# Rows by token from the first experts on: expert results combined and normed by token, residuals of feed-forward blocks added by the vector engine, the last attention by token

## The chip, the cores and the metric

The kernel runs on one core of one Trainium2 chip. The metric is device time in microseconds (us), as the median of several executions. TensorE (PE) multiplies matrices, VectorE (DVE), ScalarE (ACT) and GpSimd (POOL) work on tiles, and SyncE (SP) issues most DMAs. An indirect DMA (a gather or scatter of rows by index) is issued by POOL.

## The reference, cut to what matters

Eight sequences of 256 tokens with 128 channels (2048 tokens) go through eight sublayers; each is followed by an addition of its input and a layer norm.

```python
x = _layernorm(x + rglru(x)); x = _layernorm(x + local_attention(x)); x = _layernorm(x + mamba(x))
x = _layernorm(x + _L1_ffn_ref(x, ...))     # 32 experts, one per token
x = _layernorm(x + _L2_attn_ref(x, ...))    # chunked attention, below
x = _layernorm(x + _L2_ffn_ref(x, ...))     # 8 routed experts, two per token, and a shared one
x = _layernorm(x + _L3_attn_ref(x, ...))    # causal attention with 16 heads of four types
x = _layernorm(x + _L3_ffn_ref(x, ...))     # x @ w_eff.T + bias, w_eff ternary

def _L1_ffn_ref(x, ...):
    ...
    out_tok = jnp.where(accepted[:, None], out_tok * gate[:, None], 0.0)
    return (xt + out_tok).reshape(B, S, H)

def _L2_attn_ref(x, ...):
    # _layernorm here has a scale g and a bias b per channel
    def _mha(x, wqs, wks, wvs, pw, pb, g, b):
        ...
        return _layernorm(out @ pw + pb + x, g, b)
    def _ffn(x, w1, b1, w2, b2, g, b):
        h = jax.nn.relu(x @ w1 + b1)
        return _layernorm(h @ w2 + b2 + x, g, b)
    # la: heads within chunks of 32 tokens; sa: the same across chunks
    x = _mha(x, la...); x = _ffn(x, lf...); x = regroup(x)
    x = _mha(x, sa...); x = _ffn(x, pf...); return regroup_back(x)

def _L2_ffn_ref(x, ...):
    ...
    routed = jnp.zeros_like(xf).at[dispatch.reshape(-1)].add(contrib.reshape(-1, h))
    shared = jax.nn.silu(x @ sg) * (x @ su) @ sd
    return shared + SCALE * routed.reshape(b, s, h)
```

Since the first experts' sublayer returns x + g·out and is added to x again, the norm there is of 2x + g·out.

## The kernel before, in words

A tensor lies in SBUF either by channel (128 partitions are the channels, tokens run along the row) or by token (128 partitions are tokens, `z[128, 2, 128]` for one sequence). Matmuls contract over partitions, so they want their input by channel. A norm over channels is a norm along the row when a tensor lies by token; when it lies by channel the mean needs a matmul.

- `layernorm_steps` (L426 to L456) norms a tensor by channel. Its short form makes the centred tensor by one matmul with `centre` (tile ln), ACT squares it, a second matmul with `mean` gives the variance in the same tile, ACT forms exp(-0.5·ln(var + eps)) (ln_rs, two instructions of 256 columns) and DVE multiplies. Its form in steps has ln_mean (PE), ln_xc (DVE, L446), ln_sq (ACT, L448), ln_var (PE), ln_rs (ACT, L453 and L454) and the product (DVE, L456), with a `yield` between groups.
- `normed` (from L1240) norms by token: per 128 tokens DVE's bn_stats (L1246) and bn_aggr (L1247), then two ACT instructions of two columns (rs, L1249 and L1250), then DVE subtracts and multiplies (z, L1253). `by_channel` (L1256) transposes z back on PE (tile zt, L1259).
- `chunked` (L1348) works on the eight sequences one by one: attention la, feed-forward lf, attention sa, feed-forward pf. `on_pe` (L277) interleaves three sequences at a time: each is a generator that yields (its PE cost, the time until its next PE work can start), and the generator whose due time comes first issues next. So the order of each engine's queue is settled when the program is built.
- In `chunked`, `gather` fetches the first experts' results by token (got; three sequences ahead, issued by POOL at L1122). `combined` multiplies them by the gate (DVE, L1384), transposes them (PE, back, L1385), adds twice the layer's input by channel (DVE, xc, L1390) and norms by channel.
- `ffn` (from L1325) puts bias and residual into the output bank by PE: `add_bias` is a bf16 matmul of three bias rows against ones (out<-bias_rows), and `x` times the identity (out<-ident) adds the residual. `mha` adds its bias in the same way.
- `moe2` runs the shared expert in four parts of 512 tokens: `shared(0)` first, then the eight routed experts, then parts 1 to 3. For each of eight slices of the hidden width pg and pu are made, ACT and DVE form sh, and `acc` (by channel, 128x512) accumulates. `results(b)` takes two gathered rows per token, weights and sums them on DVE (L1551, L1553), transposes them (L1554), adds the shared part (L1556) and norms by channel to x_moe, the last attention's input. 32 gathers are issued after the experts.
- `typed` is the last attention and the ternary linear layer. A list of units (48 for the 8 sequences) gives PE's order by hand; between units up to three side steps are taken from a queue of generators: `results` of a later sequence, its projections (`typed_before`), and `after(b, o)` of a finished one: wo (L394 through `mm`), residual (L1734), norm in steps, lin, bias and residual (L1740), norm in steps, store. One PSUM bank (tag M) serves the side steps.

All matmuls made through `mm` have the line L394 in the profile. The first layers (rglru, local attention, mamba, up to about 917 us) and the first experts themselves are not touched, but for a smaller load of bias rows.

Of the kernel before, what the change touches and what calls it, by code (L numbers as in the profile page):

```python
# [21 lines left out]
P = 128  # L22
# [132 lines left out]
def _layout(d):  # L155
# [81 lines left out]
    rows = np.zeros((96, 4, P), f)  # L237
    rows[::32] = np.stack([d["L2_attn_" + n] for n in ("la_pb", "lf_b2", "sa_pb", "pf_b2")])
    out["b2"] = rows.reshape(96, 4 * P)
# [57 lines left out]
class _Kernel:  # L297
# [128 lines left out]
    def layernorm_steps(self, pool, src, dst, eps=EPS, tag="ln", steps=False):  # L426
# [29 lines left out]
        nc.vector.tensor_mul(dst, xc, rs)  # L456

# [491 lines left out]
    def route1(self, t0, t1, pools, small):  # L949
# [65 lines left out]
        nc.vector.tensor_scalar(pos, pos, float(CAP), None, ALU.is_le)  # L1015
# [104 lines left out]
    def gather(self, pool, buf, get, t, tag, bufs=None):  # L1120
        r = pool.tile([P, P], F32, tag=tag, name="got", **({"bufs": bufs} if bufs else {}))
        self.nc.gpsimd.indirect_dma_start(  # L1122
            out=r,
            out_offset=None,
            in_=buf,
            in_offset=bass.IndirectOffsetOnAxis(ap=get[:, t : t + 1], axis=0),
        )
        return r
# [9 lines left out]
    def moe1(self):  # L1138
        nc, tc = self.nc, self.tc
        E, CAP = 32, 80  # L1140
        with (
# [3 lines left out]
            full = one.tile([96, 4 * P], F32, name="bias_full")  # L1145
# [77 lines left out]
    def bias_rows(self, pool, full):  # L1223

        nc = self.nc
        self.bias = self.fc.tile([96, 4, P], BF, name="bias_rows")
        flat = self.bias.rearrange("p i d -> p (i d)")
        part = pool.tile([96, 4 * P], BF, name="bias_part")
# [96 lines left out]
    def ffn(self, x, w, name, bias, work, small):  # L1325
# [12 lines left out]
        self.add_bias(out, bias)  # L1338
        for t in range(2):
            ts = slice(t * P, (t + 1) * P)  # L1340
            for c in range(4):
                self.mm(out[:, t, :], h[:, c, ts], w2[:, c, :], False, False)
            self.mm(out[:, t, :], x[:, ts], self.ident, False, t == 1)
        z = self.normed(out[:, 0:2, :], work, small, "z")
# [3 lines left out]
    def chunked(self):  # L1348
# [7 lines left out]
        with (  # L1356
# [15 lines left out]
            def results(b):  # L1372
                got.extend(self.gather(work, self.ybuf1, self.get1, 2 * b + j, "got", 6) for j in range(2))
# [3 lines left out]

            def combined(b):

                ps = self.psum("B", "back")  # L1380
                for j in range(2):
                    t = 2 * b + j
                    r = got[t]
                    nc.vector.tensor_scalar(r, r, self.gate1[:, t : t + 1], None, ALU.mult)  # L1384
                    nc.tensor.transpose(ps[:, j * P : (j + 1) * P], r, self.ident)  # L1385
                if b + 3 < B:
                    assert len(got) == 2 * b + 6
                    results(b + 3)
                s = work.tile([P, S], F32, tag="xc", name="xc", bufs=1)
                self.combined = nc.vector.scalar_tensor_tensor(s, self.x[:, bass.ts(b, S)], 2.0, ps[:, 0:S], ALU.mult, ALU.add)  # L1390
                yield 0.3, 1.0
                x = work.tile([P, S], F32, tag="xb", name="x_moe1", bufs=5)
                self.layernorm(work, s, x)
                yield 0.9, 2.5
# [4 lines left out]
            def one_sequence(b):  # L1399
# [9 lines left out]
                x1 = affine(z, "la", "x1")  # L1409
                yield 0.3, 0.6  # L1410
                z = yield from self.ffn(x1, w[:, 0, :], "lf", 1, work, small)
                x2 = affine(z, "lf", "x2", there)
                yield 0.3, 0.6
                z = yield from self.mha(x2, self.fws[1], self.m("blk8"), 2, work, small, pools)
                x3 = affine(z, "sa", "x1")
# [3 lines left out]
                z = yield from self.ffn(x3, w[:, 1, :], "pf", 3, work, small)  # L1419
# [15 lines left out]
                self.logits(b, y, self.w1[:, 866:874], self.lg2[:, 2 * b : 2 * b + 2, :])  # L1435
                assert self.routed == b
# [9 lines left out]
            self.routed = 0  # L1446
            on_pe([one_sequence(b) for b in range(B)], 3, [self.typed_weights(prep)])
# [22 lines left out]
    def moe2(self):  # L1470
# [9 lines left out]
        with (  # L1480
# [5 lines left out]
            def shared(i):  # L1486
                cs = bass.ts(i, 512)
                acc = self.psum("S", "acc")
                for c in range(8):
# [4 lines left out]
                    i = nc.scalar.activation(h, pg, AF.Silu)  # L1494
                    if self.norm:

                        self.issue_after([i], self.norm)
                        self.norm = None
                    self.silu = i
# [317 lines left out]
```

## Time and profile before

| | us |
|---|---|
| median of 3 runs | 1902.89 (1902.8 to 1905.53) |
| the profiled execution's own time | 1898.62 |
| its span | 1896.8 |
| PE busy, granted clock | 1585.0 (84%), 0.91 |
| DVE, ACT, POOL busy | 1093.2, 1020.7, 560.4 |
| chunked attention | about 950 to 1437 |
| second experts | 1437 to 1625 |
| last attention and linear layer | 1625 to 1897 |

A row of a group names line, engine, operation, output<-input, shape and count, then the busy time in us, the mean duration of one in ns, the idle time of the engine just before these instructions, and what ended it. PEld is the load of a stationary operand. A row of a window names its bounds, its length, each engine's busy time with its number of instructions, the granted PE clock, the DMA share and GB/s. A row of the timeline has start, duration, engine, line, operation and, in brackets, the idle time before and what released it. Matmuls are pipelined, so that the duration of one is longer than the distance to the next.

### The profile page before, as it was taken

The page shows a single profiled execution, that of the slowest core. Times are in us where ns is not written, and L with a number is a line of the kernel's source. Part 1 is how long each engine was busy: PE and PEld are TensorE (multiplying, and loading weights), DVE is VectorE, ACT ScalarE, POOL GpSimd, SP SyncE. Part 2 cuts the span into 40 slices and gives each one's busy share as a digit, 9 for nine tenths or more (in the row PEclk, how much of TensorE's full clock was granted, in tenths as well). Part 3 has the DMA queues.
Part 4 walks back from the last instruction along what each step waited for, and adds up shares of the span by engine and source line. Part 5 has one row for each costly group of instructions (what it writes and reads, how often), then busy time and mean ns, then how long its engine had stood idle before and what let it go on. Part 6 is the DMA issues. An engine that isn't in the chain of part 4 may idle for free. (4 is left out here: it accounts for less than half of the span.)

```text
span 1896.8 us, 28424 instructions
## 1 busy us (share of the span) xinstructions
PE 1585.0 (84%) x10810; PEld 957.3 (50%) x10810; DVE 1093.2 (58%) x2011; ACT 1020.7 (54%) x2702; POOL 560.4 (30%) x493
## 2 busy tenths in 40 slices
PE   3678887878788778786679999999988987899997
PEld 2344554535454444343656566665554733455554
DVE  5734458687779686679234554456443222467664
ACT  4557777667767877554234455444433312365654
POOL 1324443344342423203120211111111042255452
PEclk7789998989899988888789999999998997899998
DMA  4000002111112122366300000000101310000000
GB/s 172 1 1 1 1 35 56 35 56 35 45 46 56 35 56 68 95 215 167 102 24 2 10 6 6 6 5 5 36 2 29 104 39 13 1 4 4 7 4 9
DMA packets 58328, 75.50 MB, mean 40 GB/s; under 512 B 5868, under 2 KB 35236, under 8 KB 57168
## 3 DMA queue, kind: packets, MB, share of 16 engines
q1 hardware_dynamic: 52864, 67.57, 12.2%
q0 software_dynamic: 3216, 5.07, 0.9%
q8 instruction: 85, 1.39, 0.3%
q10 hardware_dynamic: 2112, 1.05, 0.2%
q14 instruction: 51, 0.42, 0.1%
HBM read 65.46 MB, written 9.71 MB: 40 GB/s over the span
## 5 line engine op out<-in xcount | busy, mean ns | idle before, releaser
L394 PE MATMUL y<-hs,ident 128*128 128x512 f32 x256 | 152.7, 727 | 38.0 <-DVE hs L794 37.8
L793 DVE TENSOR_TENSOR_SCAN hs<-da,hs 128x1024 f32<-128x1024 f32 x64 | 153.5, 2404 | 1.8 <-ACT da L789 1.6
L475 PE MATMUL pt<-ident,e 128*128 128x128 f32 x768 | 125.6, 291 | 23.7 <-POOL e L652 12.4
L652 POOL TENSOR_TENSOR e<-e,rc 128x1024 f32<-128x1024 f32 x32 | 67.9, 2121 | 232.6 <-DVE rc L651 232.6
L1686 ACT ACTIVATE e<-sc,nm 128x128 f32<-128x128 f32 (+1 forms) x256 | 104.1, 424 | 59.8 <-DVE nm L1681 57.5
L789 ACT ACTIVATE da<-d,na 128x255 f32<-128x255 f32 x256 | 111.8, 503 | 37.6 <-DVE hs L793 18.8
L1689 POOL TENSOR_TENSOR e<-e,rc 128x1024 f32<-128x1024 f32 x48 | 91.9, 1915 | 135.7 <-DVE rc L1688 102.4
L647 ACT ACTIVATE e<-sc,nm,rn 128x128 f32<-128x128 f32 x256 | 113.4, 462 | 24.9 <-DVE nm L642 22.4
L475 PEld LDWEIGHTS pt<-ident,e 128*128 128x128 f32 x768 | 90.2, 147 | 64.1 <-issue 22.4
L1298 POOL TENSOR_TENSOR e<-e,rc 128x512 f32<-128x512 f32 x32 | 33.5, 1048 | 295.7 <-DVE rc L1297 178.9
L599 POOL TENSOR_TENSOR t<-t,t 128x512 f32<-128x512 f32 x64 | 90.9, 1421 | 95.4 <-DVE t L586 79.0
L477 ACT COPY ptsb<-pt 128x512 f32<-128x512 f32 x94 | 55.1, 587 | 96.3 <-PE pt L475 87.5
L791 DVE TENSOR_TENSOR hs<-u,bc 128x1024 f32<-128x1024 f32 x64 | 86.2, 1357 | 34.0 <-POOL u L778 29.4
L394 PEld LDWEIGHTS y<-hs,ident 128*128 128x128 f32 x256 | 53.8, 226 | 97.6 <-DVE hs L794 51.7
L1273 ACT COPY kp<-kps 128x512 f32<-128x512 f32 x128 | 74.8, 584 | 41.7 <-PE kps L394 39.8
L1122 POOL DMA_INDIRECT got<-ybuf,get x48 | 45.5, 949 | 162.2 <-DMA ybuf<-ys 116.7
L477 DVE COPY ptsb<-pt 128x512 f32<-128x512 f32 x98 | 65.6, 685 | 33.5 <-PE pt L475 33.3
L394 PE MATMUL qk<-w_local,h 128*128 128x512 f32 x128 | 71.5, 648 | 14.1 <-DVE t L586 9.7
L794 DVE TENSOR_TENSOR hs<-hs,bc 128x1024 f32<-128x1024 f32 x64 | 80.0, 1256 | 0.2
L1246 DVE BATCH_NORM_STATS2 st<-out 128x6 f32<-128x128 f32 x80 | 20.0, 288 | 93.8 <-PE out L394 86.8
L1681 DVE TENSOR_REDUCE nm<-sc 128x4 f32<-128x1024 f32 (+1 forms) x48 | 58.6, 1220 | 24.6 <-PE sc L394 24.3
L1309 ACT COPY vs<-vps 128x512 f32<-128x512 f32 x64 | 37.4, 584 | 65.6 <-PE vps L394 44.1
(394 smaller groups left out, 3899.9 us busy)
## 6 DMA issues: line engine op xcount, KB each, us to landing
bc<-xs SPq DMA_DIRECT2D x128, 256.0 KB
w_attn<-in_w_dram SPq DMA_DIRECT2D x4, 1024.0 KB
w_local<-in_w_dram SPq DMA_DIRECT2D x2, 1557.0 KB
places<-zeros SPq DMA_DIRECT2D x2, 1280.0 KB
w_moe<-in_e1gate_dram SPq DMA_DIRECT2D x8, 256.0 KB
w_moe<-in_e1up_dram SPq DMA_DIRECT2D x8, 256.0 KB
w_moe<-in_e1down_dram SPq DMA_DIRECT2D x8, 256.0 KB
w_moe<-in_e2rg_dram SPq DMA_DIRECT2D x8, 256.0 KB
```

The costliest lines, as they stand in the source:

```text
L394: return self.nc.tensor.matmul(out, lhsT, rhs, start=start, stop=stop)
L475: self.last = self.nc.tensor.transpose(pt[:, j * P : (j + 1) * P], src[:, j * P : (j + 1) * P], self.ident)
L477: self.nc.any.tensor_copy(sb.rearrange("p a b -> p (a b)"), pt)
L599: nc.gpsimd.tensor_add(t1, t1, t2)
L647: nc.scalar.activation(e[:, j, g, :], scs[:, j, g, :], AF.Exp, bias=nm[:, j, g : g + 1], scale=rq[:, j, g : g + 1], accum_out=sm[:, j, g : ...
L789: nc.scalar.activation(da[:, n, c, 1:S], d[:, c, 1:S], AF.Exp, scale=na[:, i : i + 1])
L791: nc.vector.tensor_tensor(hs, u.unsqueeze(1).to_broadcast(shp), bn, ALU.mult)
L793: nc.vector.tensor_tensor_scan(line(hs), line(da), line(hs), 0.0, ALU.mult, ALU.add)
L794: nc.vector.tensor_tensor(hs, hs, cn, ALU.mult)
L1273: nc.scalar.copy(k[:, 2 * i : 2 * i + 2, :].rearrange("p a b -> p (a b)"), ps)
L1686: nc.scalar.activation(e[:, i, :], sc[:, i, :], AF.Exp, bias=nm[:, i : i + 1], accum_out=sm[:, i : i + 1])
L1689: nc.gpsimd.tensor_tensor(e, e, rc.unsqueeze(2).to_broadcast([P, n, keys]), ALU.mult)
```

## The change

Four things are changed.

1. `combined` stays by token: gate·got + x (x by token is still in `y` from the first experts' routing; the gate is stored halved and eps divided by 4), then the new `token_norm`, then two transposes with a copy by ACT (`channels`).
2. `ffn` no longer adds bias and residual by PE. `rest` makes z·g + (b + b2) by token on POOL (two instructions), and DVE adds it to the output bank (fs); the norm reads fs.
3. The output z of the chunked layer is stored by token in DRAM (`rows_chunked`). `shared(i)` loads it into s{i}; `acc` becomes by token (h is the stationary operand, four matmuls of 128 columns for one of 512); `results` adds both gathered rows in place on DVE, norms by token and transposes after the norm.
4. `after` is by token: wo and lin with the activations as stationary operand (two matmuls of 128 columns for one of 256), norms by `token_norm`, the ternary layer's bias added by POOL, and a transpose before the store.

```diff
+    names = ("L3_ffn_bias", "L2_attn_la_g", "L2_attn_la_b", "L2_attn_sa_g", "L2_attn_sa_b", "L2_attn_lf_b2", "L2_attn_pf_b2")
+    out["rows"] = np.stack([d[n] for n in names]).astype(f).reshape(1, 7 * P)
...
+    def token_norm(self, src, dst, small, eps=EPS):
+        ...
+        for t in range(2):
+            nc.vector.bn_stats(st[:, t, :], src[:, t, :])
+            nc.vector.bn_aggr(mv[:, t, :], st[:, t, :])
+        rs = small.tile([P, 2], F32, tag="rs", name="rs")
+        nc.scalar.activation(rs, mv[:, :, 1], AF.Ln, bias=eps)
+        self.norm = nc.scalar.activation(rs, rs, AF.Exp, scale=-0.5)
+        yield
+        for t in range(2):
+            nc.vector.tensor_scalar(dst[:, t, :], src[:, t, :], mv[:, t, 0:1], rs[:, t : t + 1], ALU.subtract, ALU.mult)
+
+    def channels(self, z, dst, copy, tag="M"):
+        ps = self.psum(tag, "zt")
+        for t in range(2):
+            self.nc.tensor.transpose(ps[:, t * P : (t + 1) * P], z[:, t, :], self.ident)
+        copy(dst, ps[:, 0:S])
...
-        self.add_bias(out, bias)
         for t in range(2):
             ts = slice(t * P, (t + 1) * P)
             for c in range(4):
-                self.mm(out[:, t, :], h[:, c, ts], w2[:, c, :], False, False)
-            self.mm(out[:, t, :], x[:, ts], self.ident, False, t == 1)
-        z = self.normed(out[:, 0:2, :], work, small, "z")
+                self.mm(out[:, t, :], h[:, c, ts], w2[:, c, :], t == 0 and c == 0, t == 1 and c == 3)
+        s = work.tile([P, 2, P], F32, tag="fs", name="fs", bufs=1)
+        nc.vector.tensor_add(s, out[:, 0:2, :], add)
+        z = self.normed(s, work, small, "z")
...
+            rows = prep.tile([P, 4, P], F32, name="rows")
+            nc.sync.dma_start(rows, ...to_broadcast([P, 4 * P])...)
+            more = work.tile([P, 2, P], F32, tag="rest", name="more", bufs=3)
+            nc.sync.dma_start(more, ...to_broadcast([P, 2 * P])...)
+            for k in range(2):
+                nc.gpsimd.tensor_add(rows[:, 2 * k + 1, :], rows[:, 2 * k + 1, :], more[:, k, :])
+            def rest(z, k):
+                r = work.tile([P, 2, P], F32, tag="rest", name="rest", bufs=3)
+                for i, op in enumerate((ALU.mult, ALU.add)):
+                    nc.gpsimd.tensor_tensor(r, r if i else z, rows[:, 2 * k + i : 2 * k + i + 1, :].to_broadcast([P, 2, P]), op)
+                return r
...
             def combined(b):
-                ps = self.psum("B", "back")
+                r = got[b]
                 for j in range(2):
                     t = 2 * b + j
-                    r = got[t]
-                    nc.vector.tensor_scalar(r, r, self.gate1[:, t : t + 1], None, ALU.mult)
-                    nc.tensor.transpose(ps[:, j * P : (j + 1) * P], r, self.ident)
+                    self.combined = nc.vector.scalar_tensor_tensor(
+                        r[:, j, :], r[:, j, :], self.gate1[:, t : t + 1], y[:, t * P : (t + 1) * P], ALU.mult, ALU.add
+                    )
+                for _ in self.token_norm(r, r, small, EPS / 4):
+                    yield 0.0, 3.0
+                x = work.tile([P, S], F32, tag="xb", name="x_moe1", bufs=5)
+                self.channels(r, x, nc.scalar.copy, "B")
                 if b + 3 < B:
                     results(b + 3)
-                s = work.tile([P, S], F32, tag="xc", name="xc", bufs=1)
-                self.combined = nc.vector.scalar_tensor_tensor(s, self.x[:, bass.ts(b, S)], 2.0, ps[:, 0:S], ALU.mult, ALU.add)
                 yield 0.3, 1.0
-                x = work.tile([P, S], F32, tag="xb", name="x_moe1", bufs=5)
-                self.layernorm(work, s, x)
-                yield 0.9, 2.5
                 return x
...
+                nc.sync.dma_start(self.zrows[b * S : (b + 1) * S, :].rearrange("(t p) d -> p t d", p=P), z)
...
+                s = keep.tile([P, 4, P], F32, name=f"s{i}")
+                nc.sync.dma_start(s, self.zrows[512 * i : 512 * (i + 1), :].rearrange("(t p) d -> p t d", p=P))
...
-                    self.mm(acc, down[:, c * P : (c + 1) * P], h, c == 0, c == 7)
+                    for t in range(4):
+                        ts = slice(t * P, (t + 1) * P)
+                        self.mm(acc[:, ts], h[:, ts], down[:, c * P : (c + 1) * P], c == 0 and t == 0, c == 7 and t == 3)
...
-                nc.vector.tensor_add(s, acc, x[:, cs])
+                nc.vector.tensor_add(s, acc, s)
...
             def results(b, work):
-                ps = self.psum("M", "back")
+                z = self.rows(b)
                 for j in range(2):
                     t = 2 * b + j
...
+                    for k in range(2):
+                        i = nc.vector.scalar_tensor_tensor(z[:, j, :], got[t][k], self.gate2[:, k, t : t + 1], z[:, j, :], ALU.mult, ALU.add)
...
-                yield from self.layernorm_steps(work, s, y[:, bass.ts(b, S)], steps=True)
+                yield from self.token_norm(z, z, self.tys)
+                self.channels(z, y[:, bass.ts(b, S)], nc.vector.tensor_copy)
...
         def after(b, o):
...
-            self.mm(ps[:, 0:S], self.w3[:, 640:768], ot)
-            nc.vector.tensor_add(s, ps[:, 0:S], self.x[:, cs])
+            for t in range(2):
+                ts = slice(t * P, (t + 1) * P)
+                self.mm(ps[:, ts], ot[:, ts], self.w3[:, 640:768], t == 0, t == 1)
+            nc.vector.tensor_add(flat(s), ps, flat(self.rows(b)))
             yield
-            yield from self.layernorm_steps(work, s, s, steps=True)
-            self.mm(ps[:, 0:S], we, s)
-            nc.vector.scalar_tensor_tensor(s2, ps[:, 0:S], self.v("bias"), s, ALU.add, ALU.add)
+            yield from self.token_norm(s, s, small)
+            self.channels(s, st, nc.scalar.copy)
+            nc.gpsimd.tensor_tensor(s, s, self.bias3.unsqueeze(1).to_broadcast([P, 2, P]), ALU.add)
             yield
-            yield from self.layernorm_steps(work, s2, s2, steps=True)
-            nc.sync.dma_start(self.out[:, cs], s2)
+            for t in range(2):
+                ts = slice(t * P, (t + 1) * P)
+                self.mm(ps[:, ts], st[:, ts], we, t == 0, t == 1)
+            nc.vector.tensor_add(flat(s2), ps, flat(s))
+            yield
+            yield from self.token_norm(s2, s2, small)
+            self.channels(s2, s3, nc.scalar.copy)
+            yield
+            nc.sync.dma_start(self.out[:, cs], s3)
```

## The prediction

> **What bounds the kernel now.** I read the page's busy table first, then the windows over the three stretches that the change touches, then the groups of the operations that it takes out, and last the order of time at the two places where the tensor engine stands.
>
> ```profile
> PE 1585.0 (84%) x10810; PEld 957.3 (50%) x10810; DVE 1093.2 (58%) x2011; ACT 1020.7 (54%) x2702; POOL 560.4 (30%) x493
> ```
>
> ```profile
> core 0: us, PE busy (x) PEld busy (x) DVE busy (x) ACT busy (x) POOL busy (x), PEclk, DMA share, GB/s
> 1700.00:1750.00 50.00, 49.08 (x365) 30.23 (x365) 33.70 (x62) 29.14 (x118) 29.26 (x18) 1.00 0.01 4
> 950.00:1437.00 487.00, 441.98 (x4718) 296.86 (x4718) 232.16 (x751) 214.57 (x495) 76.33 (x76) 0.95 0.03 10
> 1437.00:1625.00 188.00, 166.80 (x554) 86.95 (x555) 49.53 (x114) 52.17 (x96) 43.11 (x42) 0.93 0.16 47
> 1625.00:1897.00 272.00, 253.00 (x1760) 150.25 (x1759) 171.60 (x308) 147.30 (x612) 127.72 (x76) 0.95 0.02 5
> ```
>
> The stretches are the chunked attention (950 to 1437), the second experts (to 1625) and the last attention (to 1897). PE is busy 91%, 89% and 93% of them, and 98% in the middle of the last (the 1700 row); DVE only 48%, 26% and 63%, 67% in that row. So PE's instruction stream sets the time there, and work taken off PE counts if DVE, which gets it, stays clear of PE's pace.
>
> ```profile
> L394 PE MATMUL acc<-sh,w_shared 128*128 128x512 f32 x64 | 37.4, 667 | 8.7 <-DVE sh L1500 8.4 <-issue 0.3
> L394 PE MATMUL out<-w_ffn,fh 128*128 128x128 f32 x256 | 35.2, 278 | 0.0
> L394 PEld LDWEIGHTS out<-w_ffn,fh 128*128 128x128 f32 x256 | 32.5, 194 | 1.6 <-ACT fh L1335 0.2 <-issue 0.2
> L394 PE MATMUL ln_mean<-s,mean 128*128 128x256 f32 x48 | 16.9, 437 | 10.9 <-DVE s L1556 9.8 <-DVE s L1740 0.6 <-DVE s L1734 0.5
> L394 PE MATMUL ln_var<-ln_sq,mean 128*128 128x256 f32 x48 | 16.8, 433 | 5.7 <-ACT ln_sq L448 5.7
> L394 PE MATMUL out<-bias_rows,onesb 96*128 96x256 bf16 x32 | 8.8, 280 | 0.3 <-DVE oh L1055 0.3
> L394 PE MATMUL out<-ident,x_la 128*128 128x128 f32 x32 | 6.2, 275 | 0.0
> L454 ACT ACTIVATE ln_rs<-ln_rs 128x256 f32<-128x256 f32 x24 | 10.0, 418 | 0.5
> L1246 DVE BATCH_NORM_STATS2 st<-out 128x6 f32<-128x128 f32 x80 | 20.0, 288 | 93.8 <-PE out L394 86.8 <-PE out L1427 7.0
> ```
>
> An fp32 matmul is two records, a transpose or a bf16 matmul one; so 48 ln_mean records are 24 matmuls. The means are latencies of pipelined records. What a matmul costs the stream is start to start: where nothing waits, the trace has successive records at 430 ns (512 columns), 216 (256), 112 (128), transposes at about 135 with a group's slower first one, the bias at 119, an ln_mean or ln_var matmul 528 for its two records, and ln<-xc and ln<-ln_sq 446 and 449.
>
> ```profile
> 957.72 0.28 DVE L1384 TENSOR_SCALAR got<-got,gate 128x128 f32<-128x128 f32 x1 [7.23 <-DMA got<-ybuf,get]
> 961.49 0.94 POOL L1122 DMA_INDIRECT got<-ybuf,get  x1 [0.30 <-issue]
> 966.45 0.29 DVE L1384 TENSOR_SCALAR got<-got,gate 128x128 f32<-128x128 f32 x1 [0.96 <-DMA got<-ybuf,get]
> 966.99 0.41 DVE L441 TENSOR_TENSOR x_moe<-ln,ln_rs 128x256 f32<-128x256 f32 x1
> 967.71 1.06 PE L394 MATMUL kps<-x_moe,la_kq 128*128 128x256 f32 x2
> ```
>
> These are the start of the chunked stage: gathers land 1.25 us apart, DVE takes them in order, and sequence 0's x_moe (its rs ready at 964.7) stands behind other sequences' gathers until 966.99; PE begins at 967.71.
>
> **The change, part by part.**
>
> Chunked, PE. Two bias matmuls per sequence go: 16 x 0.119 = 1.9 us. Residuals through ident go: 32 matmuls x 2 x 0.112 = 7.2. In combined, both ln matmuls go and the two back transposes become two zt: 0.895 per sequence, counted for sequences 3 to 7, which lie inside the stream: 4.5. Sum 13.6. PE was filled 91%; I let 85% through: **-11.6**.
>
> What DVE gets: 16 fs adds at 0.415 (the row of L1734, PSUM plus SBUF, 256 wide), minus z read from SBUF (0.289, L1384) instead of PSUM (0.403, L1253), 32 x 0.114; +3 us. Combined: two scalar_tensor_tensor (0.34), two bn_stats (0.288), two aggr (0.17), two subtract-multiply (0.289) for two multiplies, xc and x_moe: +0.8, eight times. DVE goes from 232 to 241 of some 473: 51%. Its instructions lie in the latency that the other two interleaved sequences cover; if that cover is gone, 0.42 more per FFN. Only the last sequence is exposed, at 1417 to 1437: 0.42 more for its fs, 0.45 less for its ident matmuls: nothing. The bank `out` is free after fs, earlier than after z.
>
> POOL gets 32 rest operations, nearest row 0.72 to 0.73 us (L1634, same size), 23 us on 76 of 487. A rest pair starts with z and takes 1.5; its fs add comes a zt, an affine, eight W1 matmuls, relu and 16 or more matmul records later, over 4 us. So it is hidden unless POOL's queue is behind: ahead may be two gathers (2.5 us) and one or two e (1.05 each). If all stood together, 1 to 2 us late for each of the five FFNs behind gathers: at most +10, of which the other two sequences hide some. I take nothing (0 to +10). The gathers of b+3 now wait for PE's zt after the norm, where they waited for PE's back; both are long before use.
>
> Chunked, start. The norm of sequence 0 needs no PE and comes in DVE's order behind the fourth gather (about 961.6) instead of the sixth one's neighbours; stats, rs, two multiplies, zt, copy: kps at about 964.5 for 967.7. **-3**; ends 0 and -4.5. Next late is then the gathers of sequences 1 and 2, which still end at 968.
>
> Second experts. acc takes h as the stationary operand, four 128-column matmuls for one of 512: 4 x 112 = 448 for 430 per record, 64 times: **+1.2**. The Trainium skill (TensorE: Matmul & The Clock Gate, "Back-to-back issue gap") speaks against this: in a sustained stream of loads and matmuls it has about 81 ns at 128 columns and 131 at 512, so four narrow cost 2.5 times one wide. Scaled to our 430 that is 64 x 0.43 x 1.5 = +40, and the whole change would lose. I take the trace: out<-w_ffn is exactly this shape, 256 with a load each, and runs at 112. The load already waits for sh today, so no prefetch is lost.
>
> The residual comes as rows through DRAM: on SP eight 128 KB stores, four 256 KB loads, and three row broadcasts. The stores wait for z; behind them on SP stand w_shared's weights and later the gathers' places, whose own waits are later. s0 is needed only after eight triples of 2.83 us (22 us). Nothing; if s0 or a weight were late, a few us. Three table loads fewer of 1.28, near results(0), where PE stands some 18 us between 1552 and 1581: **-1** (0 to -4). That stall belongs to the 32 gathers and stays.
>
> Last attention, PE. 48 ln matmuls go; two (results(0)) lie in the stall and four in the tail: 42 x 0.528 = -22.2. Back's 16 transposes become 48 zt: 28 more in the stream x 0.135 = +3.8. wo and lin in halves: +0.3. Sum -18.1; with 85%: **-15.4**.
>
> DVE per sequence: four scalar_tensor_tensor, six stats, six aggr, six multiplies, a copy, two adds = 7.1 us for 5.1 of today: +16 in all, 172 to 188 of some 253, 74%; in the 1700 row 33.7 becomes about 37 of 46.5, 79%. ACT loses 24 squares and 24 pairs of wide ln_rs (1.22 together) for 24 narrow pairs (0.41, by L1249) and 16 copies (0.37): -14. POOL +0.73 per sequence for s+bias3. The Trainium skill (Perfetto Trace Analysis, "Optimizing Scalar/DVE Operations") warns that GpSimd shares an SBUF read port with DVE, so that work given to both may not run side by side. The row: got (L1553), two SBUF sources, has median 342 ns but maximum 1983, and an x_moe multiply 2.15 us beside e; the other 16 multiplies of that kind 426 at most. By the rule the 30 us of new POOL work would hold DVE up to 30; by the rows, where one in ten is hit, 3. I take the rows.
>
> Tail. Each norm was ln_mean, ln_xc, ln_sq, ln_var, ln_rs twice, s; from 1881.61 to 1894.04 the chain takes 12.4. After: ot 0.42, wo 0.75, add 0.43, norm (stats and aggr 0.92, rs 0.48, multiplies 0.59), zt 0.4, copy 0.4, lin 0.9, add 0.43, norm 2.0, zt 0.45, copy 0.4, issue 0.7: about 9.3. **-3.1**.
>
> Sum: -11.6 -3 +1.2 -1 -15.4 -3.1 = -32.9. Profiled execution 1898.6 (span 1896.8), so 1865.7; it ran 4.3 below the median 1902.9, so as a median **1870.0**.
>
> **Rivals.**
>
> (a) The freed PE time comes back as waits, DVE being 74 to 79% busy and in order, so half or less of the two stream terms stays: -32.9 + 13.5 to 20 gives 1883 to 1890. For: today ln_var waits 5.7 us for ACT. Against: PE's waits in the last attention sum to 19 of 272.
>
> (b) Slower: the multiply of a token norm stands in DVE's order behind softmax reductions (nm, 1.22 us each), while zt, right behind it in PE's order, stops all of PE. 24 norms; two reductions ahead each time cost 24 x 2.4 = 59, so 1870 + 59 = 1929; it turns the result from 1.4 us per norm (33/24). For: multiply and zt are in one side step. Against: today's multiply and lin are too, and PE waited for it 1.8 us in all, twice.
>
> (c) The weight loads of acc are not hidden: +40 by the rule above, 1909. Against: the w_ffn rows.
>
> (d) The change doesn't do what it says: the bias matmuls stay for the two attentions by design; that the others go is in the code. No weight.
>
> **How the numbers follow.** Main case 0.70: 1855 to 1882. (a) 0.14: 1882 to 1899. (b) 0.09 and (c) 0.03, with mixtures about zero 0.04. Measurement tells 0.2% (3.8 us) from no change. Faster 0.82, same 0.05, slower 0.13. The range takes the main case and most of (a): 1855 to 1897.
>
> **What would show it.** Groups fs and rest; 128-column acc records near 112 start to start with no more idle before them; kps near 964.5; the chunked stretch about 15 us shorter, the last attention about 18; PE's share there still above 91%; DVE near 74%. Wrong if zt waits for DVE over 1 us per norm, if fs waits for rest, or if acc's triples exceed 2.95 us.

## The result, and the profile after

| | before | after |
|---|---|---|
| median of 4 runs, us | 1904.16 (1902.8 to 1905.53) | 1922.6 (1918.37 to 1925.72) |
| ratio | | 1.0111, 95% interval 1.0095 to 1.0126 |
| span of the profiled execution, us | 1896.8 | 1923.0 |

The change makes the kernel 1.1% slower; 1.7% faster was forecast. By marks in PE's stream (first kps, first acc, last acc, end of the span), the stages went like this:

| stage | before, us | after, us | difference | forecast |
|---|---|---|---|---|
| first py to first kps (start of the chunked stage) | 39.2 | 37.1 | -2.1 | -3 |
| chunked, first kps to first acc | 474.9 | 470.7 | -4.2 | -11.6 |
| second experts, first to last acc | 182.7 | 191.5 | +8.8 | +0.2 |
| last attention with its tail, from the last acc | 271.6 | 292.3 | +20.7 | -18.5 |

The remaining +2.9 lies ahead of the first py, in layers whose work was not changed; it moves by several us from one execution to the next, so stages are compared between marks and not by absolute time.

The page's busy table of the changed kernel, and its windows over the three stages and over the same 50 us as before (the last three columns are the granted PE clock, the DMA share and GB/s):

```profile
PE 1556.0 (81%) x10858; PEld 958.9 (50%) x10858; DVE 1133.0 (59%) x2157; ACT 1000.2 (52%) x2689; POOL 587.6 (31%) x535
```

```profile
core 0: us, PE busy (x) PEld busy (x) DVE busy (x) ACT busy (x) POOL busy (x), PEclk, DMA share, GB/s
968.30:1439.20 470.90, 428.52 (x4605) 282.14 (x4605) 244.14 (x808) 208.33 (x490) 94.50 (x102) 0.97 0.04 12
1439.20:1630.70 191.50, 161.15 (x732) 101.02 (x732) 47.14 (x100) 45.96 (x90) 43.12 (x42) 0.93 0.19 50
1630.70:1923.00 292.30, 240.53 (x1733) 150.12 (x1731) 198.08 (x397) 136.97 (x606) 132.39 (x84) 0.91 0.02 5
1700.00:1750.00 50.00, 44.31 (x304) 28.08 (x305) 32.37 (x66) 25.21 (x112) 23.23 (x16) 0.86 0.01 4
```

PE is 29 us less busy over the whole span, so the work did come off it. But the span grew: PE is 82% busy in the last attention where it was 93%, and 89% where it was 98% in the row from 1700. The granted clock there is 0.86 where it was 1.00.

PE's longest waits in the last attention (engine, output, line, what was waited for: us in total, times, longest), and the instruction behind the first, with its shortest, median and longest duration in ns:

```profile
PE zt L479 <- DVE s L473: 41.0, 24, 2.8
PE pt L499 <- POOL e L1734: 3.0, 2, 2.8
```

```profile
L473 DVE TENSOR_SCALAR s<-s,mv,rs x48: 315/345/2041, 1587.5 to 1917.1; 128x128 f32<-128x128 f32 x48
```

```profile
L473 DVE TENSOR_SCALAR s<-s,mv,rs 128x128 f32<-128x128 f32 x48 | 44.8, 975 | 4.2 <-ACT rs L470 3.0
```

The multiply of the token norm (subtract mean, multiply by rs) takes 345 ns at the median, yet 975 in the mean: 20 of the 48 take over 500 ns. These 20 fall in 20 of the 24 norms of two multiplies each, one held in each. The timeline shows what such a one does:

```profile
1725.13 0.17 DVE L1733 RECIPROCAL rc<-sm 128x4 f32<-128x4 f32 x1
1725.22 2.15 DVE L473 TENSOR_SCALAR s<-s,mv,rs 128x128 f32<-128x128 f32 x2
1725.38 1.90 POOL L1734 TENSOR_TENSOR e<-e,rc 128x1024 f32<-128x1024 f32 x1 [4.70 <-DVE rc L1733]
1726.03 0.27 PE L479 MATMUL zt<-ident,s 128*128 128x128 f32 x1
1727.42 0.33 PE L479 MATMUL zt<-ident,s 128*128 128x128 f32 x1 [1.12 <-DVE s L473]
```

DVE's reciprocal rc releases POOL's e, and the next two instructions of DVE are the multiplies. The first starts before e has begun and takes 318 ns; the second is caught by e and ends at 1727.37, 84 ns after it. Of the other held ones, each ends 81 to 84 ns after an e too. The coincidence is not chance: rc starts e, and 17 of the 20 pairs of multiplies stand directly behind rc in DVE's order, the other three two to four places behind it. The four norms that met no e had none held. Three waits of zt in PE's order, of 1.1 to 2.9 us, follow in most sequences.

The groups that answer to those of before (acc, and what is new on DVE and POOL), from the changed kernel's groups by form:

```profile
L396 PE MATMUL acc<-w_shared,sh 128*128 128x128 f32 x256 | 38.6, 296 | 28.5 <-DVE sh L1545 28.2 <-PE pg L396 0.4
L1368 DVE TENSOR_TENSOR fs<-out,rest 128x256 f32<-128x256 f32 x16 | 6.8, 424 | 41.2 <-PE out L396 40.8
L1418 POOL TENSOR_TENSOR rest<-z,rows 128x256 f32<-128x256 f32 x16 | 11.7, 732 | 99.0 <-DVE z L1278 92.8 <-DVE th L1628 6.3
```

fs waits for PE's out, never for rest: that cover held. acc waits 28 us for sh, where it waited 8.4. The timeline in the stall beside the 32 gathers shows these waits:

```profile
1544.14 1.02 PE L396 MATMUL pg<-x_chunked,w_shared 128*128 128x512 f32 x2
1552.87 0.69 DVE L1545 TENSOR_TENSOR sh<-sh,pu 128x512 f32<-128x512 f32 x1 [10.64 <-remote]
1553.61 2.07 PE L396 MATMUL acc<-w_shared,sh 128*128 128x128 f32 x8 [8.45 <-DVE sh L1545]
1558.34 1.12 PE L396 MATMUL pg<-x_chunked,w_shared 128*128 128x512 f32 x2 [1.10 <-issue]
1577.40 2.08 PE L396 MATMUL acc<-w_shared,sh 128*128 128x128 f32 x8 [17.94 <-DVE sh L1545]
```

PE first stands 13 us after the first gather; in the kernel before it did 18 to 21 us after it, and stood 10 us less. PE is not the engine that stops first: pu, the later input of that sh, was done at 1544.30, yet DVE starts sh 8.6 us later, and the profile names no engine of this core as its releaser.

### The profile page after: what moved, and what is told of

It is laid out like the page before. It is cut to its first block, busy times and chain, and to the rows that moved or that the text cites. A ratio compares the mean times of both kernels' runs of the same rounds, so it can differ in the third digit from the quotient of the medians.

```text
span 1923.0 us, 28706 instructions
## 1 busy us (share of the span) xinstructions
PE 1556.0 (81%) x10858; PEld 958.9 (50%) x10858; DVE 1133.0 (59%) x2157; ACT 1000.2 (52%) x2689; POOL 587.6 (31%) x535
## 4 chain that ended last, share of the span: by engine, by line
PE 52%; DVE 19%; ACT 12%; issue 7%; POOL 6%; another core or an unknown queue 2%; DMA 2%; SPq 0%; DVEq 0%; POOLq 0%; ACTq 0%
PE vps L396 7%; PE kps L396 6%; PE sc L396 5%; PE pt L499 4%; PE o L396 4%; PE out L396 3%; PE pu L396 3%; PE pg L396 3%; DVE hs L817 3%; ACT e L671 2%; PE y L396 2%; DVE hs L818 2%; DVE s L473 2%; DVE hs L815 2%
## 5 line engine op out<-in xcount | busy, mean ns | idle before, releaser
L396 PE MATMUL y<-hs,ident 128*128 128x512 f32 x256 | 148.5, 710 | 37.6 <-DVE hs L818 37.2
L1545 DVE TENSOR_TENSOR sh<-sh,pu 128x512 f32<-128x512 f32 x32 | 22.0, 688 | 90.7 <-PE pu L396 47.3
```

Source lines behind the costliest of these rows:

```text
L396: return self.nc.tensor.matmul(out, lhsT, rhs, start=start, stop=stop)
```

## The experiments

The groups of runs fell on different chips. On some of them the kernel before takes 1845 to 1847 us instead of 1900: its chunked stage takes 445 us instead of 475, and there is no stall beside the gathers (second experts 160 us in every kernel). The changed kernel itself was not run on such a chip. So ratios are to the kernel before in the same group, and stage times are compared on like chips. The following experiments are of two theories of the last attention: **port** (a multiply cannot run while POOL works on e) and **queue** (rival b as the prediction worded it: softmax reductions stand ahead of the multiplies).

**psum_norm.** The norm's source is the PSUM bank instead of a copy in SBUF; the instructions stay. Their order on DVE was meant to stay too, but in the built kernel it did not quite, as the trace below shows.

```diff
-            nc.vector.tensor_add(flat(s), ps, flat(self.rows(b)))
+            nc.vector.tensor_add(ps, ps, flat(self.rows(b)))
             yield
-            yield from self.token_norm(s, s, small)
+            yield from self.token_norm(ps.rearrange("p (t d) -> p t d", t=2), s, small)
# the same for lin's sum; in results the second sum of each half goes to PSUM
-                        i = nc.vector.scalar_tensor_tensor(z[:, j, :], ...)
+                        i = nc.vector.scalar_tensor_tensor((zp if k else z)[:, j, :], ...)
```

> Theory 1 (port): a DVE tensor_scalar that reads and writes SBUF cannot run while POOL works on e; it ends some 80 ns after POOL does. With the norm's source in PSUM the same instruction is never held: all 48 near 0.40 us (now mean 0.98), PE's waits of zt for it fall from 41 us to below 8, the kernel gets 28 to 36 us faster than the changed one: 1887 to 1895. Theory 2 (queue, rival b as the prediction worded it): the multiplies are late because softmax reductions stand ahead of them in DVE's order. That order and the number of instructions stay, so zt still waits about 40 us and the time stays at 1918 to 1926.

> The norm's source in PSUM, once more, to stand beside the others of this group. Theory 1 (port): 0.984 to 0.990 of before; last attention 245 to 249 us. If this chip has the stall beside the gathers, the second experts stay at 191 us, since nothing of them is changed against the changed kernel.

Measured 1819.78 us, 0.9857 of before (0.9837 to 0.9877) on the chip without the stall, and 1873.73 us, 0.9879 (0.984 to 0.9919) on one with it: the first is 27 us faster than the kernel before, the second 27. Of the second run, these are the multiplies, PE's waits for them, and the window of the last attention:

```profile
L473 DVE TENSOR_SCALAR s<-zs,mv,rs x16: 399/405/411, 1580.8 to 1801.8; 128x128 f32<-128x128 f32 x16
L473 DVE TENSOR_SCALAR s<-wo,mv,rs x16: 400/405/412, 1673.3 to 1859.3; 128x128 f32<-128x128 f32 x16
L473 DVE TENSOR_SCALAR s<-lin,mv,rs x16: 394/398/410, 1679.9 to 1863.5; 128x128 f32<-128x128 f32 x16
```

```profile
PE zt L479 <- DVE s L473: 14.0, 10, 2.6
```

```profile
1623.90:1869.80 245.90, 219.49 (x1733) 136.69 (x1731) 178.35 (x393) 138.58 (x611) 132.21 (x84) 0.98 0.02 6
```

No multiply is held any more: 22 of the 48 run wholly inside an e, at 399 to 411 ns. The waits fall by 27 us, and the stage by 47.7 (245.9 against 293.6 on the same kind of chip), 23.6 below the kernel before. The gain on the changed kernel is larger than the 28 to 36 us expected; the clock, under order_psum below, accounts for it. The queue theory, which expected no gain, falls. The waits "below 8 us" were missed, and the trace shows by what:

```profile
1706.86 2.22 DVE L1598 SCALAR_TENSOR_TENSOR s<-got,gate,s 128x128 f32<-128x128 f32 x2
1707.02 1.91 POOL L1735 TENSOR_TENSOR e<-e,rc 128x1024 f32<-128x1024 f32 x1 [1.97 <-DVE rc L1734]
1709.00 0.72 DVE L473 TENSOR_SCALAR s<-lin,mv,rs 128x128 f32<-128x128 f32 x2
1709.78 0.44 PE L479 MATMUL zt<-ident,s 128*128 128x128 f32 x2 [1.57 <-DVE s L473]
```

In this kernel two sums of gathered rows (L1598, two inputs in SBUF) have come to stand between rc and the multiplies in five sequences. The second of them is held by e for 1.98 us, and the multiplies, not held themselves, come late behind it. These five waits of 1.57 us are 7.8 of the 14.0 us; the two norms of the tail are another 5.1. So most of what the source in PSUM left inside the stream is the same hold on another instruction.

**no_e.** POOL's normalisation of e in the last attention is left out.

```diff
-        nc.gpsimd.tensor_tensor(e, e, rc.unsqueeze(2).to_broadcast([P, n, keys]), ALU.mult)
```

> Leaves out the normalisation of e by POOL in the last attention (48 instructions of 1.9 us), so the softmax is not divided by its sum. Theory 1: nothing of length is left on POOL there, the 48 multiplies take 0.34 us each, zt waits fall below 6 us, and the waits of pt for e (3 us) go too: 35 to 45 us faster than the changed kernel. Theory 2: DVE's queue is the same, zt waits stay near 40 us, and only the 3 us of pt go.

1810.86 us in a single run, beside 1847 for the kernel before; last attention 240.0 us.

```profile
PE zt L479 <- DVE s L473: 11.7, 10, 2.3
```

```profile
L473 DVE TENSOR_SCALAR s<-s,mv,rs x48: 315/342/348, 1525.8 to 1802.6; 128x128 f32<-128x128 f32 x48
```

With the source in SBUF as in the changed kernel but no e on POOL, the longest multiply takes 348 ns. So neither operand place nor DVE's queue holds it by itself; POOL's e does. The 11.7 us of zt waits that are left here, with nothing held, are five of 1.15 us and two of over 2 us in the tail.

**side_first.** Same instructions, with the side steps of a unit issued ahead of its softmax.

```diff
-            if 0 <= i - 1 < n:
-                es[i - 1] = self.typed_softmax(...)
             for _ in range(2):
                 ...
+            if 0 <= i - 1 < n:
+                es[i - 1] = self.typed_softmax(...)
```

> Same instructions; in the loop over the units the two side steps are issued ahead of the softmax of the unit instead of behind it, so a norm's multiplies stand ahead of rc, whose end starts POOL's e. Theory 1: how many multiplies meet an e changes; those ahead of rc meet only the e of the unit before, if it still runs. 10 to 30 us faster, with the held ones (about 1.9 us) fewer than 24 and the others at 0.34. Theory 2: the reductions no longer stand ahead, zt waits nearly go whether or not POOL runs, 30 us faster and more, and no multiply takes over 0.4 us.

1821.46 us, 0.9867 of before (0.9846 to 0.9888); last attention 251.5 us.

```profile
L473 DVE TENSOR_SCALAR s<-s,mv,rs x48: 333/344/1673, 1524.2 to 1813.0; 128x128 f32<-128x128 f32 x48
```

3 of 48 multiplies are held instead of 20. The zt waits are 18.8 us. The source is still in SBUF and POOL still does all its e: what made the change slower is the place of the multiplies right behind rc. Seven of the 32 sums of gathered rows (L1597) are held here too, for up to 1.99 us, as in psum_norm. This run alone would fit both theories, as more than one thing moves.

**order_psum.** Both at once.

> Both at once: the norm's source in PSUM and the side steps ahead of the softmax. Theory 1: with the source in PSUM no multiply is held, so the order has nothing left to mend but the 14 us of zt waits that remain in the kernel with PSUM alone; gain over that one 0 to 8 us: 0.981 to 0.986 of before. Theory 2 (queue): those 14 us are DVE's order, and go with it: 10 us or more.

1891.7 us, 0.9956 (0.9945 to 0.9967): by the ratios worse than either alone. In the profiled execution (1898.72 us, one of the two longest of 20) the last attention takes 262.5 us, with 18.9 us of zt waits in 9 waits:

```profile
1634.40:1896.90 262.50, 230.99 (x1733) 143.30 (x1731) 176.83 (x392) 140.49 (x612) 132.16 (x84) 0.94 0.02 5
```

Both theories missed. The total of the waits is only 5 us above psum_norm's, but PE is 11.5 us longer busy with the same 1733 records. The difference is in the shape of the waits. Here five sequences have one of 2.4 to 2.7 us, in psum_norm's second run five have one of 1.57; in both it stands behind a held sum of gathered rows, and here PE comes to zt some 0.9 us sooner after e has begun. Around four of the five of 2.4 us and over the granted clock goes to 0.5, for 3.41 or 6.83 us; about the five of 1.57 us in psum_norm it does not. In all, the clock is at half for 32 us of this stage, against 8 in psum_norm (its second run, in the tail alone) and 55 and 59 in the two profiles of the changed kernel. Half the clock for 24 us more would cost up to 12 us of PE time, by estimate, which fits the 11.5.

**before_again, after_again.** The two kernels once more, in the group with order_psum.

> The kernel before, for its trace on the chip that the other kernels of this group run on: chunked stage (first kps to first acc), second experts (to the last acc) and last attention are to be compared stage by stage. If the stall beside the gathers at the end of the second experts belongs to the chip and not to the program, that stage takes 160 us here too where the first chip had 183; if the change made the stall, it stays at 183.

> The changed kernel, for its time and trace on the same chip. Theory 1 (port): its last attention is the same 292 us with 41 us of zt waits, its second experts are as long as those of before but for 1.2 us, so it comes to between 1.000 and 1.006 of before, and 1.4 to 2.2% above the kernel with the norm's source in PSUM. If the second experts' 9 us came from the change: 1.011 of before again.

before_again 1901.52 us in a single run (the group's runs of before have a median of 1900.18); after_again 1919.56 us, 1.0122 (1.0088 to 1.0155). Stages of before and after: start 39.1 and 33.7, chunked 474.6 and 469.9, second experts 183.2 and 191.6, last attention 269.5 and 293.6. So the second experts' 8.4 us do come from the change on such a chip, and "1.000 to 1.006" was missed by them. On the chip without the stall the stage takes 160.4 us with the second experts of before (chunk_only) and 159.5 with those of the change.

**acc_wide.** acc as one matmul of 512 columns again.

```diff
-                    for t in range(4):
-                        ts = slice(t * P, (t + 1) * P)
-                        self.mm(acc[:, ts], h[:, ts], down[:, c * P : (c + 1) * P], c == 0 and t == 0, c == 7 and t == 3)
+                    self.mm(acc, down[:, c * P : (c + 1) * P], h, c == 0, c == 7)
```

> The changed kernel with acc as one matmul of 512 columns again in place of four of 128 (the shared part is then by channel where the rest is by token, so the transposition is left out). Theory A: in the stall beside the gathers PE waits for its own instructions, and with four times the acc instructions it runs dry sooner; then PE first stands some 20 us after the first gather instead of 13, and the second experts take 183 us instead of 191. Theory B: the stall grew by what results(0) or the loads of rows do: 13 us and 190 us stay. If the chip shows no stall at all: 158.5 us, 1.2 less than with four.

1917.81 us in a single run. Second experts 181.6 us, and PE first stands 20 us after the first gather, not 13:

```profile
1553.22 1.02 PE L396 MATMUL pu<-x_chunked,w_shared 128*128 128x512 f32 x2
1555.60 1.13 PE L396 MATMUL pg<-x_chunked,w_shared 128*128 128x512 f32 x2 [1.36 <-issue]
1564.16 2.08 PE L396 MATMUL acc<-sh,w_shared 128*128 128x512 f32 x2 [7.43 <-DVE sh L1545]
```

So the four matmuls in place of one bring 9 to 10 us on such a chip. Of these 1.2 are their own, as the sum had it: undisturbed triples of pg, pu and acc are 2.87 us apart with four and 2.83 with one. The rest is a longer stall. That PE runs out of its own instructions, as theory A says, is not shown: in the rows here and in those of the changed kernel above PE's long waits are for DVE's sh, which DVE starts late. Why more matmuls make the stall begin sooner stays open.

**psum_paced, before_paced; psum_spread, before_spread, and the two once more.** The gathers after the experts wait for the products of the shared expert's slices: a pair for each slice, or for every three.

```diff
-            got = [[self.gather(keep, ybuf, self.get2[:, k], t, f"got{k}{t}") for k in range(2)] for t in range(NT)]
+            fetch(), fetch()     # four gathers; then, in the loops over the slices:
+                fetch(self.paced)
```

> PSUM as above; and of the 32 gathers after the experts 28 are issued two at a time, each pair after the product of one slice of the shared expert (2.9 us), instead of all at 1.25 us apart. If the burst of gathers holds up the other traffic (theories A and B alike), the stall goes and the second experts come to 160 to 165 us, 25 us off the kernel with PSUM alone. If the stall is a fixed price per gather it stays and is only spread. On a chip without the stall: the same time within 2 us.

> The kernel before with the same pacing of the gathers and nothing else. Where the stall exists: 20 us faster than before if the burst makes it, the same if each gather has its price. On a chip without the stall: the same within 2 us.

> The norm's source in PSUM, and the gathers after the experts far apart: four at once, then two per three slices of the shared expert (8.6 us), the last twelve in the last attention. Theory A (the burst keeps PE's own instructions from coming): no stall is left, second experts 159 to 165 us where the stall exists, against 181 with pairs every 2.9 us and 191 with the burst; the kernel 15 to 20 us faster than with those pairs. Theory B (a price per gather, or a stall at this place in the program whatever the gathers do): 180 to 191 us again. On a chip without the stall: as the kernel with PSUM alone, within 2 us.

> The kernel before with the gathers spread in the same way. Theory A: second experts 160 to 166 us where the stall exists, 15 to 20 us faster than before. Theory B: the same as before within 3 us, or as with pairs every 2.9 us (176 us, 7 us faster). On a chip without the stall: the same.

> As psum_spread, once more, for a chip that has the stall. Theory A: second experts 159 to 165 us there, 0.975 to 0.980 of before. Theory B: 180 to 191 us, 0.982 to 0.988 of before. Where the chip has no stall: 159 us and 0.984, which tells nothing.

> As before_spread, once more. Theory A: second experts 160 to 166 us on a chip with the stall. Theory B: 176 to 183 us.

| kernel | us | ratio (95%) | second experts, us |
|---|---|---|---|
| psum_paced | 1867.61 | 0.9837 (0.9809 to 0.9864) | 180.6 (psum_norm 190.9) |
| before_paced | 1894.08 | 0.9961 (0.9943 to 0.9978) | 176.2 (before 183.2) |
| psum_spread, no stall on the chip | 1816.9 | 0.9839 (0.9817 to 0.9861) | 159.5 |
| before_spread, no stall on the chip | 1847.82 | 1.0004 (0.999 to 1.0018) | 160.7 |
| psum_spread_2 | 1873.5 | 0.9842 (0.9805 to 0.9878) | 182.8 |
| before_spread_2 | 1898.84, a single run | | 176.5 |

The experiment did not do what it meant to. Only the second gather of a pair was given the wait, and the traces show the first 24 to 28 of the 32 gathers 1.25 us apart, as in the burst; only the rest came later. On the chips with the stall the burst was 29 to 33 us long where it was 38.8, and the stage became 7 to 10 us shorter. That a shorter burst makes a shorter stall fits this. The times of the last pair lie in theory B's ranges, but theory A's 159 to 165 us was not tested, so neither is decided, and the stall's cause stays open. psum_paced and the two psum_spread runs have ratios of 0.9837 to 0.9842; their intervals overlap that of psum_norm, so pacing adds nothing that is clear of noise to the kernel with PSUM alone.

**combined_only, chunk_only.** Before with only combined by token; and before with both chunked parts.

> Before, with only the results combined and normed by token in the chunked stage (no change to the feed-forward residuals, second experts, last attention). With both chunked edits the gain was 5.7 us of the 14.6 forecast. If the residual edit carries it (9.1 us of PE work taken off), this kernel is within 3 us of before; if the start and the 4.5 us of PE work of combined carry it, 5 to 8 us faster than before; if the held multiplies of combined (up to 0.75 us, 8 of 16) cost more than it saves, slower than before.

> Only the parts in the chunked stage: combined by token, residuals of the feed-forward blocks by POOL and DVE; second experts and last attention as before. If the chunked steps of the prediction hold, 15 us faster than before: 1889. If the trace of the changed kernel is right that most of it is given back at the stage's end: 4 to 8 us faster than before, 1896 to 1900. If the chunked parts cost something: over 1904.

combined_only 1897.66 us, 0.9988 (0.9974 to 1.0002): start 35.2 us for 39.1, chunked 475.8 for 474.6. chunk_only 1841.35 us, 0.9964 (0.9952 to 0.9977), 5.7 us: so the chunked parts are a gain, of the smaller size. On that kind of chip start and chunked take 37.1 and 442.5 us, against 41.0 and 445.3 in before_spread, which has these stages as before. combined is worth its earlier start and nothing in the stream; that the residuals carry the rest is a difference of the two runs, as they were not run alone.

## Why the prediction was wrong

**The failed step** is the sentence "By the rule the 30 us of new POOL work would hold DVE up to 30; by the rows, where one in ten is hit, 3. I take the rows." It looked for new work on POOL that would meet DVE. For the new work the 3 us were about right: eight multiplies of combined ran beside rest and took 428 to 753 ns where the shortest takes 311, some 2 us in all. What counted was the e that was already there, 91 us of it, met by new work on DVE, a meeting that the sum put at nothing. 20 of the 48 multiplies were held, one in each of 20 norms, which is 30 us more than their 0.34 us each; 27 of PE's 41 us of waits go with the hold. That the rule's figure was 30 as well is chance.

The rows were also read too mildly. In the last attention before, e held 4 of the 16 instructions of L1553 and 2 of the 16 of L1551 for 1.92 to 1.98 us, and 6 of the 8 x_moe multiplies (2.15 us once, 755 to 937 ns else, for 424). With the 16 multiplies s (L456) of 426 ns at most that is 12 of 56, not one in ten. And a share taken from there says little about the new places: the 16 have both inputs in SBUF too, but none of them stood where an e had over 0.1 us still to run. The question that was not asked is what stands ahead of the multiplies on DVE and whom that releases.

The section of the Trainium skill that states it best was not used: SBUF — State Buffer, "Who interferes with whom", describes the pair of ports that DVE and GpSimd share as an exclusive lock, held for a whole instruction. DVE needs it in a mode with two ports, which tensor_scalar can enter, or with two SBUF inputs while GpSimd reads SBUF, and whichever comes first has it. Here the trace agrees: the tensor_scalar from SBUF to SBUF and the scalar_tensor_tensor with two SBUF inputs are held, the latter to 147 ns after e's end; those that read PSUM, bn_stats (276 to 295 ns beside e, 259 to 296 else) and the reductions (1224 to 1225 ns beside e, 1193 to 1225 else) run beside e at their usual time.

**A second term was missing**: what a wait of PE costs beyond itself. Between psum_norm and the changed kernel lie 47.7 us in the last attention, of which 25.4 are PE's idle time (51.8 against 26.4) and 22.3 its busy time at the same number of records (241.8 against 219.5), while the clock was granted at half for 59 us instead of 8. By estimate half of those 50 us, 25, is what the half clock can cost.

**Rival (b)** named the right wait and the right place (24 norms, multiply and zt in one side step, decisive from 1.4 us per norm; measured 41/24 = 1.7) with the wrong reason (reductions ahead; it is rc that stands there) and 9 in 100. Its price was 59; measured were 41 us of waits and 48 us of time. **Rival (a)** came true in part, in the chunked stage.

**Chunked, -11.6: mis-sized.** The step that failed is "I let 85% through". PE's busy time fell by 11.0 us between the marks (8.8 in before_again and after_again, 7.1 in before_spread and chunk_only), where the sum had 13.6; but PE's idle time rose by 6.9 (4.1, 4.4), so a fifth to a third of the sum came through. One wait rises in all three pairs: zt for z, from 5.5 to 9.4 us in the first; it stands at 9.1 in combined_only too. The last sequence's second attention starts 5.9 us earlier relative to the first kps, and from there, alone, it gives back 1.7.

**Start, -3:** -2.1 to -5.7 over the runs. **rest, nothing:** right, fs waits for PE's out alone. The multiply from SBUF takes 0.34 us, not the 0.289 read off L1384, which only multiplies; nothing hung on that. **acc, +1.2 and not the +40 of the rule:** right by the records (2.87 for 2.83 us a triple), wrong in the stage, where the stall took 8 more: the prediction's "stays" failed there. **Rival (c)** did not occur. **Tail, -3.1:** right for the chain, which takes 9.0 to 9.1 us from ot to the store's issue (9.3 forecast) where it took 11.9 to 12.5. But from that issue to the end of the span it is 4.6 us where it was 2.8, which no step had and whose cause was not looked for; so 1.1 to 1.6 us are left.

**Last attention without the hold:** psum_norm comes to -23.6 against before on a like chip, with the tail, where -18.5 was forecast; so the stream term was sound. A part of the 23.6 is clock, which the sum did not have: at half for 20.6 us of this stage in before_again, 8.4 in psum_norm, by estimate some 6 us, which leaves 17 to 18. That its total, 27 us below before, lies near the forecast of 33 is in part luck: the 8 us too few in the chunked stage and the 8 too many in the second experts are partly made up by the clock and an earlier start.

## What to carry to other kernels

Before work is moved from PE to DVE, list for each new DVE instruction what stands just ahead of it in DVE's order and what that releases on GpSimd. Here, of every two multiplies from SBUF to SBUF that met a long GpSimd operation, one was held to its end (20 of 20 norms). Reading the source from PSUM (0.40 us for 0.34) or issuing the step ahead of the release mended it for the multiplies; but the order on DVE has to be looked at again afterwards, since other instructions with two SBUF inputs had come to stand behind the release, and doing both was worse than either. A share of slow instances taken from one place of the order says nothing about another place; and where PE is the bound, a wait of 2 us can have a stretch of half clock behind it.

## What the runs showed of the hardware

- A held DVE instruction ends 81 to 84 ns (tensor_scalar, changed kernel) or 147 to 150 ns (scalar_tensor_tensor with two SBUF inputs, kernel before and changed) after the GpSimd operation that held it.
- The held ones have their source in SBUF: 22 of 48 multiplies with the source in PSUM ran wholly inside an e at 399 to 411 ns (psum_norm).
- PE's granted clock went to 0.5, mostly for 3.41 or 6.83 us, around 5 of 6 waits of 2.8 us in the last attention of the changed kernel ahead of its tail, around 3 of 5 of 1.8 us, around its waits of 1.57 and 1.46 us, and around none of its 7 between 1.1 and 1.44 us; five waits of 1.57 us in psum_norm had none. So the length of a wait alone does not decide it.
- Chips differ by 3% on the same program (1845 to 1847 and 1900 us): chunked stage 445 against 475 us, second experts 160 against 183, last attention 269 against 270 to 272.
